# Seven quarter products in place of eight for a pointwise convolution inside a fused attention and cluster block

## The chip, the cores and the metric

One Trainium2 chip, one of its cores, float32 throughout. The metric is the device time of one execution in microseconds, and the times given are medians of repeated executions. The kernel is a two-layer network over four images of 256 channels and 64x64 pixels.

## The reference, cut to what matters

Layer 0 is self attention over the 4096 pixels of an image. Layer 1 is a cluster block followed by an MLP; the change touches only the end of layer 1:

```python
y = x + ls1 * cluster(group_norm(x), ...)
hdn = conv1x1(group_norm(y), mlp_w1, mlp_b1)          # 256 -> 1024
hdn = conv1x1(gelu(hdn), mlp_w2, mlp_b2)              # 1024 -> 256
y = y + ls2 * hdn
z = relu(batch_norm(y * dw_w, dw_g, dw_b, dw_m, dw_v))
z = relu(batch_norm(conv1x1(z, pw_w), pw_g, pw_b, pw_m, pw_v))   # 256 -> 256: the pointwise convolution
```

A `conv1x1` is a matrix product of a weight matrix with the pixels: here 256x256 by 256x4096 for an image.

## The kernel before

**Tiling.** An image's 4096 pixels go in eight blocks of 512 (`nb`), its channels in two halves of 128 partitions (`KC`). The third image leaves its last block over; it is worked off in the last image's cluster stage (`late_block`). TensorE is fed a stationary 128x128 weight tile and a moving tile of 256 or 512 columns, and each float32 product appears in the profile as two MATMUL rows.

**The order.** The whole body is under a manual schedule: each engine runs its instructions strictly in the order in which the program emits them, and waits on other engines by semaphore. The MLP of an image is the double loop at the end of `mlp`: for each block `nb`, for `j` in 0 to 3, `first(nb, j)` makes a quarter of the hidden layer and the second layer of the previous `j` is woven into it. The second layer is a Python generator, `second_by_seven`; `first` pulls products out of it at four points, `mo(0)` to `mo(3)`, and the tuple `slots` says how many at each. After a step without attention scores, `slots` is (0, 2, 2, 3); after one with, (3, 1, 2, 1).

**Strassen-like quarters.** Both MLP layers are already done with seven quarter products in place of eight: the weights and the 512-column operand are each cut in four (256 columns at a time), sums of the quarters are made, and seven products suffice. In `first`, `norm` makes the scaled input (VectorE, L1168) and four sums of its quarters (L1184 to L1187; on GpSimd, except for block 0). Three pairs of PSUM banks, `p`, `q` and `r`, take 2, 3 and 2 products. They come from a pool of two such pairs (`ps_s`), so a pair must have been read out before the next but one group can write. VectorE adds the products (`plus`, L1290), ScalarE copies one (L1307) and applies gelu (L1287).

**The second layer, product by product** (L1247). Call the hidden quarters of step `j` h1 to h4. Product 1 is w3 by h4, 2 is a12 by h3, 3 is a11 by h1; then GpSimd has rewritten the quarters, and 4 is w7 by h4, 5 is s1 by h2, 6 is s2 by h1, 7 is a22 by h3. GpSimd's four rewrites are h4 = h2 + h4 (L1252) and h2 = h2 − h1 (L1253), emitted after product 1, and h1 = h1 − h4 (L1256) and h3 = h1 + h3 (L1257), emitted after product 3. With (0, 2, 2, 3) products 1 and 2 come at `mo(1)`, 3 and 4 at `mo(2)`, 5 to 7 at `mo(3)`.

**The pointwise convolution.** `finish(nb)` adds the second layer's result to y, and two relus on ScalarE (L1336, emitted at the next block's `j` = 1) write the convolution's input over the block's own sums, `pairs[nb][:, 1]`. `last(nb)` (L1194) then runs at `j` = 2 of the next block: four 512-column products (L1206), two into each of two banks of one `ps_s` pair, two relus on ScalarE (L1215) and two output transfers on SyncE's queue (L1218). In an image's last block the previous block's convolution is called in the middle of `first` and uses two other banks; the last block's own convolution comes after the loop.

**What stands beside.** The sums for the next block, `norm(nb + 1)`, are scaled at `j` = 1; their GpSimd part is kept in `behind` and emitted inside the second layer of `j` = 1, after product 3's rewrites. Scores of the next image's attention are put in at `j` = 3 of each block (`score`; not in the last image, which has no next), and their running maxima run on VectorE as 128x512 maxima of two SBUF tiles (L372), called by `rest()` after `first` for `j` other than 1 and before it for `j` = 3.

Of the kernel before, what the change touches and what calls it, by code (L numbers as in the profile page):

```python
# [8 lines left out]
F32 = mybir.dt.float32  # L9
# [36 lines left out]
def attention_then_cluster_block(  # L46
# [977 lines left out]
    def late_block(b, y, gab):  # L1024
# [44 lines left out]
        def second(j, c):  # L1069
            if j == 0:  # L1070
                held["a", c] = ps_m.tile([P, NB], F32, tag="m", name=f"mol_{b}_{c}")
            nc.tensor.matmul(
                held["a", c],
                own_w["w2"][:, j, c * P : (c + 1) * P],
                hidden(j),
                start=(j == 0),
                stop=(j == HID // P - 1),
            )
            if j == HID // P - 1:
                t = work.tile([P, NB], F32, tag=f"w{c}", bufs=1, name=f"tl_{b}_{c}")  # L1080
                nc.scalar.activation(t, held["a", c], AF.Identity, scale=par("ls2", c))
                nc.gpsimd.tensor_tensor(held["y"][:, 0, c], held["y"][:, 0, c], t, ALU.add)
                nc.scalar.activation(
                    held["x"][:, 1, c],
                    held["y"][:, 0, c],
                    AF.Relu,
                    scale=dw_d[:, c : c + 1],
                    bias=dw_e[:, c : c + 1],
                )

        def last(c, k):
            if k == 0:
                held["p"] = ps_m.tile([P, NB], F32, tag="m", name=f"pwl_{b}_{c}")
            x = held["x"]
            nc.tensor.matmul(
                held["p"],
                wpw_s[:, k, c * P : (c + 1) * P],
                x[:, 1, k],
                start=(k == 0),
                stop=(k == KC - 1),  # L1100
            )
# [35 lines left out]
    def mlp(b, ys, stats2, fill, nxt, blocks, turned):  # L1137
# [15 lines left out]
        w3_s = swap.tile([P, h_n, P], F32, tag="mix", name=f"w2_3_{b}")  # L1153
# [8 lines left out]
        def norm(nb, eng):  # L1162


            pairs[nb] = pr = spool.tile([P, 2, KC, NB], F32, tag="s", name=f"xn2_{b}_{nb}")

            def scaled(k):
                nc.vector.tensor_scalar(  # L1168
                    pr[:, 0, k, :],
                    block(ys, k, nb),  # L1170
                    ga[:, k : k + 1],
                    gb[:, k : k + 1],
                    ALU.mult,
                    ALU.add,
                )


            e, f, g, h = quarters(pr[:, 0])
            t2, t4, t3, _ = quarters(pr[:, 1])
            scaled(0)  # L1180
            scaled(1)

            def factors():
                eng.tensor_tensor(f, f, e, ALU.subtract)  # L1184
                eng.tensor_tensor(t2, h, f, ALU.subtract)
                eng.tensor_tensor(t3, e, t2, ALU.subtract)
                eng.tensor_tensor(t4, t2, g, ALU.subtract)  # L1187

            return factors

        def quarters(t):
            return t[:, 0, :HB], t[:, 0, HB:], t[:, 1, :HB], t[:, 1, HB:]

        def last(nb, beside=False):  # L1194
            zs = pairs.pop(nb)

            if beside:
                ps = [
                    ps_m.tile([P, NB], F32, tag="m", name=f"pw{c}_{b}_{nb}") for c in range(KC)
                ]  # L1200
            else:
                two = ps_s.tile([P, 2, NB], F32, tag="s", name=f"pw_{b}_{nb}")
                ps = [two[:, c, :] for c in range(KC)]
            for c in range(KC):
                for k in range(KC):
                    nc.tensor.matmul(  # L1206
                        ps[c],
                        wpw_s[:, k, c * P : (c + 1) * P],
                        zs[:, 1, k, :],
                        start=(k == 0),  # L1210
                        stop=(k == KC - 1),
                    )
            for c in range(KC):
                o_s = zs[:, 0, c, :]
                nc.scalar.activation(  # L1215
                    o_s, ps[c], AF.Relu, scale=pw_s[:, c : c + 1], bias=pw_e[:, c : c + 1]
                )
                nc.sync.dma_start(out=ob[:, c, nb * NB : (nb + 1) * NB], in_=o_s)  # L1218

        norm(0, nc.vector)()  # L1220
        if nxt:
            nxt.q_block(0, nc.sync)

# [12 lines left out]
                    stop=(j == h_n - 1 and i != c),  # L1236
                )

        def second_by_seven(nb, acc, hs, j):


            h1, h2, h3, h4 = quarters(hs)
# [3 lines left out]
            def q(bank, half, a, t, start=False, stop=False):  # L1246
                return nc.tensor.matmul(  # L1247
                    bank[:, half * HB : (half + 1) * HB], a[:, j], t, start=start, stop=stop
                )

            yield q(x, 1, w3_s, h4, one)
            nc.gpsimd.tensor_tensor(h4, h2, h4, ALU.add)  # L1252
            nc.gpsimd.tensor_tensor(h2, h2, h1, ALU.subtract)  # L1253
            yield q(x, 0, a12_s, h3, stop=end)
            yield q(y, 0, a11_s, h1, one, end)
            nc.gpsimd.tensor_tensor(h1, h1, h4, ALU.subtract)  # L1256
            nc.gpsimd.tensor_tensor(h3, h1, h3, ALU.add)  # L1257
# [15 lines left out]
        def first(nb, j, todo, slots, meanwhile=lambda: None):  # L1273


            e, f, g, h = quarters(pairs[nb][:, 0])
            t2, t4, t3, _ = quarters(pairs[nb][:, 1])
            hs = work.tile([P, 2, NB], F32, tag=("t", "acc")[j % 2], bufs=1, name=f"hs_{b}_{nb}_{j}")
            h1, h2, h3, h4 = quarters(hs)
            act = AF.Gelu_apprx_tanh  # L1280
            lo, hi = pvc("b1", P, j), pvc("b1", P, j + 4)

            def banks(n):
                return ps_s.tile([P, 2, NB], F32, tag="s", name=f"h{n}_{b}_{nb}_{j}")

            def gelu(dst, src, bias):
                nc.scalar.activation(dst, src, act, bias=bias)  # L1287

            def plus(dst, ps, term):
                nc.vector.tensor_tensor(dst, ps, term, ALU.add)  # L1290
# [5 lines left out]
                    next(todo, None)  # L1296

            def product(out, w, x):
                nc.tensor.matmul(out, w[:, j * P : (j + 1) * P], x, start=True, stop=True)  # L1299


            mo(0)
            ps = banks("p")
            p, u = ps[:, 0, :HB], ps[:, 1, :HB]
            product(p, W_A, e)
            product(u, w_abcd, t2)
# [5 lines left out]
            product(q, W_CD, f)  # L1312
            product(u, w_bac, t3)
            product(v, w_bcd, h)
            plus(h3, u, h2)
            plus(h4, q, h3)
            gelu(h4, h4, hi)
            plus(h2, q, h2)
            plus(h2, v, h2)
            gelu(h2, h2, lo)  # L1320
            mo(2)
            meanwhile()
            ps = banks("r")
            p, u = ps[:, 0, :HB], ps[:, 1, :HB]
            product(p, W_B, g)
            product(u, W_D, t4)
            plus(h1, p, h1)
            gelu(h1, h1, lo)
            plus(h3, u, h3)
            gelu(h3, h3, hi)  # L1330
            mo(3)
            return hs

        def finish(nb, acc):
            def relu(c):
# [38 lines left out]

        hooks, drips, behind, maxima = [], [], [], []

        def hook():
            while hooks:  # L1380
# [4 lines left out]
                maxima.pop(0)()  # L1385

        acc, todo, slots = None, iter(()), (0,) * 4

        at = {(u, 3): u for u in range(7)} | {(7, 2): 7}
        if blocks < NBLK:  # L1390
# [2 lines left out]
        for nb in range(blocks):  # L1393
            end = nb == blocks - 1
            for j in range(4):
                if j == 3:
                    rest()
                pw = (lambda: last(nb - 1, True)) if end and j == 2 else lambda: None
                hs = first(nb, j, todo, slots, pw)
                if j != 1:  # L1400
                    rest()
# [166 lines left out]
```

## Time and profile before

| What | Value |
|---|---|
| Median of three executions | 3380.36 us (3377.95 to 3381.68) |
| The profiled execution, its own time | 3380.63 us |
| Span of its instructions | 3378.8 us |
| Granted TensorE clock, mean | 0.997 |
| TensorE busy | 3320.6 us |
| VectorE, ScalarE, GpSimd busy | 2151.6, 1659.6, 1833.4 us |
| DMA, mean over the span | 21 GB/s |
| Pointwise convolution L1206, MATMUL rows in all | 248 |
| One MLP block in the steady stretch (693.38 to 722.79) | 29.41 us, TensorE busy 29.27 |

The span is what the trace shows from the first to the last instruction; the execution's own time has 1.8 us more around it. Times inside the trace are microseconds from the span's start. MATMUL rows overlap, so the time of a product is read from the distance between starts, not from a row's length. Idle time of an engine other than TensorE costs nothing unless TensorE comes to wait for it. A trace can lack a few matmul records.

### The profile page before, as it was taken

What the parts mean: (1) busy time and instruction counts of PE and PEld (TensorE: products, weight loads), DVE (VectorE), ACT (ScalarE), POOL (GpSimd) and SP (SyncE); (2) the same over time, 40 slices, a digit from 0 to 9 for tenths busy, and PEclk for the clock granted to TensorE, in tenths of its full rate; (3) what the DMA queues carried; (4) which work ended last, traced back from release to release, by engine and by line L of the source; (5) the groups of instructions that cost most, each with busy time, mean ns of one, the idle gap of its engine ahead of it and who ended that gap; (6) DMA issues with size and microseconds to landing.
All of it is one profiled execution on the core that took longest, in us unless ns stands there. A gap on an engine that the chain in (4) does not pass through costs nothing.

```text
span 3378.8 us, 34064 instructions
## 1 busy us (share of the span) xinstructions
PE 3320.6 (98%) x12184; PEld 1778.9 (53%) x12184; DVE 2151.6 (64%) x3381; ACT 1659.6 (49%) x2184; POOL 1833.4 (54%) x1255
## 2 busy tenths in 40 slices
PE   8999999999999999999999999999999999999999
PEld 4434445777533344577744334467763344346786
DVE  4667664666666766466666676646656766765654
ACT  5545543444555554344455555434445555544444
POOL 2655666354365666545535566554534676573553
PEclk9999999999999999999999999999999999999999
DMA  2000002000000000100000000010000000010000
GB/s 71 13 13 11 15 7 86 4 13 19 26 13 13 13 13 22 71 4 19 19 22 13 10 13 13 22 70 4 19 26 13 13 13 13 10 39 1 13 19 26
DMA packets 43098, 70.95 MB, mean 21 GB/s; under 512 B 9680, under 2 KB 18480, under 8 KB 42928
## 3 DMA queue, kind: packets, MB, share of 16 engines
q1 hardware_dynamic: 38064, 61.94, 5.5%
q10 hardware_dynamic: 4608, 6.30, 0.8%
q8 instruction: 96, 1.57, 0.2%
q14 instruction: 74, 0.61, 0.1%
q0 software_dynamic: 256, 0.52, 0.1%
HBM read 43.46 MB, written 16.89 MB: 18 GB/s over the span
## 4 chain that ended last, share of the span: by engine, by line
PE 91%; DVE 7%; ACT 1%; issue 1%; DMA 0%; SPq 0%; ACTq 0%; DVEq 0%
PE av L473 53%; PE sc L359 8%; PE mo L1247 8%; PE hq L1299 4%; PE pw L1206 3%; PE hp L1299 3%; PE hr L1299 3%; PE vp L310 2%; PE fv L857 2%; DVE hs L1290 2%; PE mo L1231 1%; DVE x L1345 1%; DVE top L372 1%; PE op L978 1%; PE qp L329 0%
## 5 line engine op out<-in xcount | busy, mean ns | idle before, releaser
L473 PE MATMUL av<-s,v 128*128 128x512 f32 x4096 | 1819.2, 598 | 0.6 <-ACT s L463 0.6
L468 POOL TENSOR_TENSOR acc<-acc,s 128x1024 f32<-128x1024 f32 x448 | 1057.4, 2360 | 537.7 <-ACT s L463 518.9
L473 PEld LDWEIGHTS av<-s,v 128*128 128x128 f32 x4096 | 759.1, 190 | 1044.8 <-issue 1034.5
L463 ACT ACTIVATE s<-s 128x1024 f32<-128x1024 f32 x512 | 540.3, 1057 | 592.2 <-DVE s L460 549.5
L460 DVE TENSOR_TENSOR s<-s,mb 128x1024 f32<-128x1024 f32 x512 | 595.6, 1206 | 18.7 <-ACT mb L444 16.3
L381 DVE TENSOR_TENSOR top<-sc,top 128x1024 f32<-128x1024 f32 x196 | 239.4, 1222 | 374.6 <-PE sc L359 374.4
L1287 ACT ACTIVATE hs<-hs,pv_s 128x256 f32<-128x256 f32 x496 | 230.9, 503 | 350.3 <-DVE hs L1290 350.3
L1247 PE MATMUL mo<-hs,w 128*128 128x256 f32 x1512 | 385.9, 381 | 0.0
L377 ACT COPY s<-sc 128x1024 f32<-128x1024 f32 x224 | 224.9, 1004 | 225.7 <-PE sc L359 225.7
L1247 PEld LDWEIGHTS mo<-hs,w 128*128 128x128 f32 x1512 | 281.2, 190 | 59.0 <-issue 15.2
L359 PE MATMUL sc<-q,k 32*128 32x512 f32 x2048 | 294.7, 640 | 0.4 <-ACT s L382 0.4
L384 DVE TENSOR_TENSOR top<-sc,top 128x1024 f32<-128x1024 f32 x196 | 240.1, 1225 | 72.2 <-ACT s L377 59.5
L382 ACT COPY s<-sc 128x1024 f32<-128x1024 f32 x224 | 227.1, 1014 | 66.2 <-DVE top L379 36.2
L465 POOL TENSOR_TENSOR acc<-s 128x1024 f32<-128x1024 f32 x32 | 75.3, 2352 | 327.0 <-ACT s L463 327.0
L1252 POOL TENSOR_TENSOR hs<-hs 128x256 f32<-128x256 f32 x108 | 78.5, 727 | 305.7 <-PE mo L1247 201.5
L1290 DVE TENSOR_TENSOR hs<-hq,hs 128x256 f32<-128x256 f32 x496 | 198.6, 421 | 68.9 <-PE hq L1299 58.8
L1290 DVE TENSOR_TENSOR hs<-hp,hs 128x256 f32<-128x256 f32 x124 | 52.4, 423 | 267.4 <-ACT hs L1307 267.4
L359 PEld LDWEIGHTS sc<-q,k 32*128 32x128 f32 x2048 | 81.7, 182 | 182.5 <-issue 128.4
L1299 PE MATMUL hr<-xn,w 128*128 128x256 f32 x496 | 127.5, 379 | 0.3 <-DVE hs L1290 0.3
L310 PE MATMUL vp<-wv_s,x 128*128 128x256 f32 x512 | 123.4, 387 | 0.2 <-ACT v L318 0.2
L1206 PE MATMUL pw<-xn,wpw_s 128*128 128x512 f32 x248 | 112.1, 594 | 1.5 <-ACT xn L1336 1.5
L1256 POOL TENSOR_TENSOR hs<-hs 128x256 f32<-128x256 f32 x108 | 80.6, 746 | 57.6 <-PE mo L1247 55.7
(236 smaller groups left out, 3281.0 us busy)
## 6 DMA issues: line engine op xcount, KB each, us to landing
x<-in_x SPq DMA_DIRECT2D x32, 512.0 KB, 6.7
out<-xn SPq DMA_DIRECT2D x62, 256.0 KB, 2.1
w<-in_w SPq DMA_DIRECT2D x8, 1024.0 KB, 10.1
mr<-row_mx SPq DMA_DIRECT2D x28, 256.0 KB, 3.1
rden<-row_rd SPq DMA_DIRECT2D x28, 256.0 KB, 3.1
q<-q ACTq DMA_DIRECT2D x96, 64.0 KB, 2.0
mix<-in_wfv SPq DMA_DIRECT2D x8, 192.0 KB, 8.1
q<-q SPq DMA_DIRECT2D x24, 64.0 KB, 2.0
```

The source lines that it names most:

```text
L359: nc.tensor.matmul(halves[r // 2][:, r % 2, :], k_s[rows, g, :], q_s[rows, :], start=True, stop=True)
L381: nc.vector.tensor_tensor(top, halves[1], top, ALU.max)
L382: nc.scalar.copy(s[:, 2:4, :], halves[1])
L384: nc.vector.tensor_tensor(top, halves[0], top, ALU.max)
L460: nc.vector.tensor_tensor(sh, sh, mxs[nb].unsqueeze(1).to_broadcast([P, 2, NB]), ALU.subtract)
L463: nc.scalar.activation(sh, sh, AF.Exp)
L468: nc.gpsimd.tensor_tensor(acc, acc, s[:, 2 * h : 2 * h + 2], ALU.add)
L473: nc.tensor.matmul(av[c], own["v"][:, RG * g + quarter, c * P : (c + 1) * P], slots[u][:, quarter, :], start=(g == 0 and quarter == 0), st ...
L1247: return nc.tensor.matmul(bank[:, half * HB : (half + 1) * HB], a[:, j], t, start=start, stop=stop)
L1287: nc.scalar.activation(dst, src, act, bias=bias)
L1290: nc.vector.tensor_tensor(dst, ps, term, ALU.add)
L1299: nc.tensor.matmul(out, w[:, j * P : (j + 1) * P], x, start=True, stop=True)
```

## The change

The pointwise convolution of most blocks is turned to seven quarter products, in the form of `first`, whose inner part is taken out as a function `seven` and used by both. A new function `pointwise(nb)` calls it at the place of `last(nb - 1)`, `j` = 2 of blocks that are neither an image's first nor its last. The convolution's stored weights are changed in place at the start (two GpSimd operations), and three sums of them are made in each image's MLP, in the tile that holds w3.

The four sums of the convolution's operand (`factors`) are emitted on GpSimd inside the second layer of `j` = 1: the first ahead of product 1, the second ahead of product 3, the other two after product 3's rewrites. The next block's four sums, which stood there, move to the second layer of `j` = 2, after product 3's rewrites. `slots` is (3, 1, 2, 1) after the `j` = 2 of a block with a convolution.

An image's last two convolutions and the carried-over block stay at eight quarters (four 512-column products). Since the stored weights are changed, each of them gets one subtraction of the operand's halves: on GpSimd for the last but one and the carried-over block, on VectorE for the last.

```diff
+    pw_q = [wpw_s[:, k, h * P : (h + 1) * P] for k in range(KC) for h in range(2)]
+    nc.gpsimd.tensor_tensor(pw_q[1], pw_q[1], pw_q[3], ALU.add)
+    nc.gpsimd.tensor_scalar(pw_q[3], pw_q[3], -1.0, None, ALU.mult)
...
+                if c:
+                    x = held["x"]
+                    nc.gpsimd.tensor_tensor(held["y"][:, 1, 0], x[:, 1, 0], x[:, 1, 1], ALU.subtract)
...
-        def last(nb, beside=False):
+        def last(nb, beside, eng):
+
             zs = pairs.pop(nb)
+            eng.tensor_tensor(zs[:, 0, 1], zs[:, 1, 0], zs[:, 1, 1], ALU.subtract)
...
-                        wpw_s[:, k, c * P : (c + 1) * P],
-                        zs[:, 1, k, :],
+                        pw_q[2 * k + c],
+                        zs[:, 0, 1] if k and c else zs[:, 1, k],
...
+        def factors(eng, src, dst):
+
+
+            e, f, g, h = quarters(src)
+            t2, t4, t3, _ = quarters(dst)
+            yield eng.tensor_tensor(f, f, e, ALU.subtract)
+            yield eng.tensor_tensor(t2, h, f, ALU.subtract)
+            yield eng.tensor_tensor(t3, e, t2, ALU.subtract)
+            yield eng.tensor_tensor(t4, t2, g, ALU.subtract)
...
+        nc.gpsimd.tensor_tensor(pw_abcd, pw_q[1], pw_q[0], ALU.subtract)
+        nc.gpsimd.tensor_tensor(pw_bac, pw_abcd, pw_q[3], ALU.add)
+        nc.gpsimd.tensor_tensor(pw_bcd, pw_q[2], pw_abcd, ALU.subtract)
...
-        def second_by_seven(nb, acc, hs, j):
+        def second_by_seven(nb, acc, hs, j, own, ahead):
...
+            if j == 1:
+                next(own, None)
             yield q(x, 1, w3_s, h4, one)
             nc.gpsimd.tensor_tensor(h4, h2, h4, ALU.add)
             nc.gpsimd.tensor_tensor(h2, h2, h1, ALU.subtract)
             yield q(x, 0, a12_s, h3, stop=end)
+            if j == 1:
+                next(own, None)
             yield q(y, 0, a11_s, h1, one, end)
             nc.gpsimd.tensor_tensor(h1, h1, h4, ALU.subtract)
             nc.gpsimd.tensor_tensor(h3, h1, h3, ALU.add)
             if end:
                 early(nb, acc)
-            if behind:
-                behind.pop()()
+            if j == 1:
+                for _ in own:
+                    pass
+            if j == 2:
+                for _ in ahead:
+                    pass
             yield q(z, 0, w7_s, h4, one)
...
+        def pointwise(nb):
+            zs = pairs.pop(nb)
+
+            outs, spent = quarters(zs[:, 1]), quarters(zs[:, 0])
+            dst = outs[0], spent[0], spent[2], outs[3]
+
+            def done(i, src):
+                c = i // 2
+                rectified(c, outs[i], src)
+
+                if i % 2 == 0:
+                    leave(nb, c, zs[:, 1, c])
+
+            ws = (pw_q[0], pw_abcd, pw_q[1], pw_bac, pw_bcd, pw_q[2], pw_q[3])
+            seven(f"{nb}_pw", ws, zs[:, 1], zs[:, 0], dst, done, iter(()), (0,) * 4)
...
-                    if nb + 1 < blocks:
-                        behind.append(norm(nb + 1, nc.gpsimd))
+                    if not end:
+                        ahead = norm(nb + 1, nc.gpsimd)
+                        if nb:
+                            own = factors(nc.gpsimd, pairs[nb - 1][:, 1], pairs[nb - 1][:, 0])
+                        else:
+                            own = iter(())
                 elif j == 2 and nb and not end:
-                    last(nb - 1)
+                    pointwise(nb - 1)
...
-                    todo = second_by_seven(nb, acc, hs, j)
-                    slots = (3, 1, 2, 1) if scored else (0, 2, 2, 3)
+                    todo = second_by_seven(nb, acc, hs, j, own, ahead)
+                    slots = (3, 1, 2, 1) if scored or j == 2 and nb else (0, 2, 2, 3)
...
-        last(blocks - 1)
+        last(blocks - 1, False, nc.vector)
```

`seven` is the old inner part of `first` with the weights, the operand, the sums and the destinations as arguments: group `p` (2 products), a ScalarE copy and one VectorE addition; group `q` (3 products), four VectorE additions and two activations; group `r` (2 products), two VectorE additions and two activations. For the convolution the activation is the relu with its scale and bias, and nothing of the second layer is woven in.

More of the change, by code (lines that the diff above doesn't have):

```diff
@@ L1096, in last @@
                 held["p"],
-                wpw_s[:, k, c * P : (c + 1) * P],
-                x[:, 1, k],
+                pw_q[2 * k + c],
+                held["y"][:, 1, 0] if k and c else x[:, 1, k],
                 start=(k == 0),
@@ L1152, in mlp @@
         nc.gpsimd.tensor_tensor(w_bcd, W_B, w_abcd, ALU.subtract)
-        w3_s = swap.tile([P, h_n, P], F32, tag="mix", name=f"w2_3_{b}")
+        few = swap.tile([P, h_n + 3, P], F32, tag="mix", name=f"w2_3_{b}")
+        w3_s, (pw_bcd, pw_bac, pw_abcd) = few[:, :h_n], (few[:, h_n + i] for i in range(3))
         nc.gpsimd.tensor_tensor(w3_s, s2_s, a12_s, ALU.add)
@@ L1175, in scaled @@
                 )
-            e, f, g, h = quarters(pr[:, 0])
-            t2, t4, t3, _ = quarters(pr[:, 1])
             scaled(0)
             scaled(1)
[L1183 to L1189, printed above, removed]
+            return factors(eng, pr[:, 0], pr[:, 1])
         def quarters(t):
             return t[:, 0, :HB], t[:, 0, HB:], t[:, 1, :HB], t[:, 1, HB:]
-        def last(nb, beside=False):
+        def last(nb, beside, eng):
             zs = pairs.pop(nb)
+            eng.tensor_tensor(zs[:, 0, 1], zs[:, 1, 0], zs[:, 1, 1], ALU.subtract)
             if beside:
@@ L1207, in last @@
                         ps[c],
-                        wpw_s[:, k, c * P : (c + 1) * P],
-                        zs[:, 1, k, :],
+                        pw_q[2 * k + c],
+                        zs[:, 0, 1] if k and c else zs[:, 1, k],
                         start=(k == 0),
@@ L1213, in last, with rectified, leave @@
             for c in range(KC):
[L1214 to L1220, printed above, removed]
+                rectified(c, zs[:, 0, c], ps[c])
+                leave(nb, c, zs[:, 0, c])
+        def rectified(c, o_s, src):
+            nc.scalar.activation(
+                o_s, src, AF.Relu, scale=pw_s[:, c : c + 1], bias=pw_e[:, c : c + 1]
+            )
+        def leave(nb, c, o_s):
+            nc.sync.dma_start(out=ob[:, c, nb * NB : (nb + 1) * NB], in_=o_s)
+        def factors(eng, src, dst):
[5 more added lines that the diff above has]
+            yield eng.tensor_tensor(t4, t2, g, ALU.subtract)
+        for _ in norm(0, nc.vector):
+            pass
+        nc.gpsimd.tensor_tensor(pw_abcd, pw_q[1], pw_q[0], ALU.subtract)
+        nc.gpsimd.tensor_tensor(pw_bac, pw_abcd, pw_q[3], ALU.add)
+        nc.gpsimd.tensor_tensor(pw_bcd, pw_q[2], pw_abcd, ALU.subtract)
         if nxt:
@@ L1259, in second_by_seven @@
                 early(nb, acc)
-            if behind:
-                behind.pop()()
+            if j == 1:
[3 more added lines that the diff above has]
+                for _ in ahead:
+                    pass
             yield q(z, 0, w7_s, h4, one)
@@ L1273, in first, with gelu, seven, banks @@
         def first(nb, j, todo, slots, meanwhile=lambda: None):
-            e, f, g, h = quarters(pairs[nb][:, 0])
-            t2, t4, t3, _ = quarters(pairs[nb][:, 1])
             hs = work.tile([P, 2, NB], F32, tag=("t", "acc")[j % 2], bufs=1, name=f"hs_{b}_{nb}_{j}")
[L1279 to L1287, printed above, removed]
+            def gelu(i, src):
+                nc.scalar.activation(
+                    src, src, AF.Gelu_apprx_tanh, bias=pvc("b1", P, j + 4 * (i > 1))
+                )
+            ws = [
+                w[:, j * P : (j + 1) * P] for w in (W_A, w_abcd, W_CD, w_bac, w_bcd, W_B, W_D)
+            ]
+            seven(f"{nb}_{j}", ws, pairs[nb][:, 0], pairs[nb][:, 1], quarters(hs), gelu, todo, slots, meanwhile)
+            return hs
+        def pointwise(nb):
[9 more added lines that the diff above has]
+            seven(f"{nb}_pw", ws, zs[:, 1], zs[:, 0], dst, done, iter(()), (0,) * 4)
+        def seven(n, ws, src, sums, dst, act, todo, slots, meanwhile=lambda: None):
+            e, f, g, h = quarters(src)
+            t2, t4, t3, _ = quarters(sums)
+            h1, h2, h3, h4 = dst
+            w_p, w_u, w_q, w_u3, w_v, w_p2, w_u4 = ws
+            def banks(i):
+                return ps_s.tile([P, 2, NB], F32, tag="s", name=f"h{i}_{b}_{n}")
             def plus(dst, ps, term):
@@ L1298, in product @@
             def product(out, w, x):
-                nc.tensor.matmul(out, w[:, j * P : (j + 1) * P], x, start=True, stop=True)
+                nc.tensor.matmul(out, w, x, start=True, stop=True)
             mo(0)
@@ L1304, in first @@
             p, u = ps[:, 0, :HB], ps[:, 1, :HB]
-            product(p, W_A, e)
-            product(u, w_abcd, t2)
+            product(p, w_p, e)
+            product(u, w_u, t2)
             nc.scalar.copy(h1, p)
@@ L1311, in first @@
             q, u, v = ps[:, 0, :HB], ps[:, 1, :HB], ps[:, 0, HB:]
-            product(q, W_CD, f)
-            product(u, w_bac, t3)
-            product(v, w_bcd, h)
+            product(q, w_q, f)
+            product(u, w_u3, t3)
+            product(v, w_v, h)
             plus(h3, u, h2)
             plus(h4, q, h3)
-            gelu(h4, h4, hi)
+            act(3, h4)
             plus(h2, q, h2)
             plus(h2, v, h2)
-            gelu(h2, h2, lo)
+            act(1, h2)
             mo(2)
@@ L1324, in first @@
             p, u = ps[:, 0, :HB], ps[:, 1, :HB]
-            product(p, W_B, g)
-            product(u, W_D, t4)
+            product(p, w_p2, g)
+            product(u, w_u4, t4)
             plus(h1, p, h1)
-            gelu(h1, h1, lo)
+            act(0, h1)
             plus(h3, u, h3)
-            gelu(h3, h3, hi)
+            act(2, h3)
             mo(3)
-            return hs
         def finish(nb, acc):
@@ L1373, in finish @@
                 hooks.append(lambda c=c: relu(c))
-        hooks, drips, behind, maxima = [], [], [], []
+        hooks, drips, maxima = [], [], []
         def hook():
@@ L1387, in mlp @@
         acc, todo, slots = None, iter(()), (0,) * 4
+        own = ahead = iter(())
         at = {(u, 3): u for u in range(7)} | {(7, 2): 7}
@@ L1397, in mlp @@
                     rest()
-                pw = (lambda: last(nb - 1, True)) if end and j == 2 else lambda: None
+                pw = (lambda: last(nb - 1, True, nc.gpsimd)) if end and j == 2 else lambda: None
                 hs = first(nb, j, todo, slots, pw)
```

## The prediction

> **What bounds the kernel now.** I read the page first: how busy each engine is, and the chain of waits that ended last.
>
> ```profile
> PE 3320.6 (98%) x12184; PEld 1778.9 (53%) x12184; DVE 2151.6 (64%) x3381; ACT 1659.6 (49%) x2184; POOL 1833.4 (54%) x1255
> ...
> PE 91%; DVE 7%; ACT 1%; issue 1%; DMA 0%; SPq 0%; ACTq 0%; DVEq 0%
> PE av L473 53%; PE sc L359 8%; PE mo L1247 8%; PE hq L1299 4%; PE pw L1206 3%; PE hp L1299 3%; PE hr L1299 3%; PE vp L310 2%; PE fv L857 2%; DVE hs L1290 2%; PE mo L1231 1%; DVE x L1345 1%; DVE top L372 1%; PE op L978 1%; PE qp L329 0%
> ...
> L1206 PE MATMUL pw<-xn,wpw_s 128*128 128x512 f32 x248 | 112.1, 594 | 1.5 <-ACT xn L1336 1.5
> ```
>
> TensorE is busy 98% of the span and 91% of the chain. So a product taken away is worth its whole time, and a wait put ahead of TensorE costs its whole time. The convolution itself is 3% of the chain. The other engines are half idle on average, which says nothing of one stage. Hence the second view, the timeline of one image's third block (nb=2), around the place where the change lands:
>
> ```profile
> 722.79 1.07 PE L1247 MATMUL mo<-hs,w 128*128 128x256 f32 x4
> 723.02 1.50 ACT L1336 ACTIVATE xn<-x,dw_e,dw_d 128x512 f32<-128x512 f32 x2
> ...
> 723.53 0.73 POOL L1252 TENSOR_TENSOR hs<-hs 128x256 f32<-128x256 f32 x1 [2.65 <-PE mo L1247]
> ...
> 724.34 0.72 POOL L1253 TENSOR_TENSOR hs<-hs 128x256 f32<-128x256 f32 x1
> ...
> 725.74 0.73 POOL L1256 TENSOR_TENSOR hs<-hs 128x256 f32<-128x256 f32 x1 [0.68 <-PE mo L1247]
> ...
> 726.54 0.73 POOL L1257 TENSOR_TENSOR hs<-hs 128x256 f32<-128x256 f32 x1
> 726.72 1.46 PE L1247 MATMUL mo<-hs,w 128*128 128x256 f32 x6
> ...
> 727.23 0.73 POOL L1184 TENSOR_TENSOR xn<-xn 128x256 f32<-128x256 f32 x1
> 727.60 2.04 DVE L372 TENSOR_TENSOR top<-top,s 128x512 f32<-128x512 f32 x2
> ...
> 728.02 3.60 PE L1206 MATMUL pw<-xn,wpw_s 128*128 128x512 f32 x8
> 728.04 1.05 POOL L1185 TENSOR_TENSOR xn<-xn 128x256 f32<-128x256 f32 x1
> ...
> 731.45 0.59 PE L1299 MATMUL hp<-xn,w 128*128 128x256 f32 x2
> ```
>
> Columns: start, duration, engine, line, operation. A product is two MATMUL rows. I call the start of the first line S (722.79). TensorE runs products 1 and 2 of the second layer at S and S+0.43, 3 and 4 at S+2.21 and S+2.64, 5 to 7 at S+3.93, S+4.36 and S+4.80 (the x6 line, 0.43 apart). GpSimd makes what they read: h4 (L1252) for product 4, h2 (L1253) for 5, h1 (L1256) for 6, h3 (L1257) for 7. h1 ends at 726.47, S+3.68, so product 6 has 0.68 us in hand; h3 ends at 727.27, S+4.48, so product 7 has 0.32. That 0.32 us is what the change spends. The separate starts show the same pattern, within 0.02 us, for nb=1 to 5 of every image; at nb=6 of the first two images products 5 to 7 are 0.43 later.
>
> [...] so I take spacings. L1252 to L1253, where the second waits for the first, is 0.80; L1257 to L1184, which does not, is 0.69. [...] beside L372 the GpSimd L1185 takes 1.05, where most of its kind take 0.73.
>
> **The change part by part.**
>
> *Removed from TensorE.* Four 512-column products take 731.45 − 728.02 = 3.43 us. Seven 256-column ones at 0.432 (the spacing of L1247 and L1299) take 3.03. Gain 0.40 us. The next hq product waits for the old 128x512 relus (23 waits on L1215, 0.08 us of TensorE each, as 733.18 to 733.69 instead of 0.43); that goes, since the new evictions are shorter and earlier. Gain 0.48 in all. It happens at nb=1 to 6 of three images and nb=1 to 5 of the third: 23 places, 11.0 us. An image's last two convolutions stay at eight quarters.
>
> *Added on GpSimd, and moved.* The four sums for the next block (L1184 to L1187) move from this stage to the next one; the pointwise operand's four take their place, but two of them are set ahead of the second layer's own. The new order in j=1's second layer is: own f, h4, h2, own t2, h1, h3, own t3, own t4. Own f reads the first relu (L1336). The two relus take 0.75 each, and the first one's record ends at 723.82, S+1.03. GpSimd follows ACT by about 0.08 (L1082 starts at 3135.93 after ACT's 3135.16+0.69). So f starts at S+1.11; h4 0.69 later, S+1.80; h2 at S+2.60 (0.80); t2 at S+3.28 (the second relu is done by S+1.73); h1 at S+3.97; h3 at S+4.77. With 0.73 each and 0.08 to reach TensorE: product 4 can start at S+2.61 (due 2.64, just in time), 5 is free, 6 at S+4.78 (due 4.36), 7 at S+5.58 (due 4.80). Everything behind product 7 in TensorE's queue slips by 0.78 us. Net for a place: 0.78 − 0.48 = +0.30.
>
> *The tie at S+4.8.* In three images VectorE starts its L372 at S+4.81, 0.04 us after h3's start by my sum. Where GpSimd starts 0.11 ahead (L1253 at 3317.57 against L1345 at 3317.68) it keeps its 0.73 and VectorE is stretched to 1.16. If VectorE is first instead, h3 waits for nearly all of one two-input read, some 0.6 (L1185 comes 0.44 after L372 and still loses 0.32). Then the slip is about 1.4, at 17 of the 23 places; the last image has no L372. I take GpSimd first; both ends go into the range.
>
> *The seven products after that.* Bank pairs: the third group needs the first one's pair, free after a ScalarE copy and a VectorE addition, 0.35 + 0.42 after the u product, and the second group's 1.30 us of products covers that. The copy overwrites e, so it waits for own t3, S+5.46 to about 6.8[...]; the first group ends at S+6.87, so nothing. VectorE gets seven additions of 0.42, 2.9 us, into an idle stretch of 4.89 (with one row less of L372, at 703.98). ScalarE gets a 0.35 copy and four 0.5 relus for two of 0.75. After them three second-layer products come first, 1.30 us, and cover the last additions. The next block's moved sums end about 4 us later than j=2's h3, still ahead of their use where a score stands between. Nothing here.
>
> *Small ones.* Last image, nb=0: no score stands between, and t2 is late. h1 stays at 3172.73, h3 3173.54, f 3174.23, t2 3175.03 to 3175.76, reaching TensorE at 3175.84; its product is due at 3175.44: +0.4 us. An image's last convolution gets a VectorE subtraction (a two-input 128x512 L372 takes 0.68 alone) behind two 1.15 us subtractions of L460: 895.17+2.3+0.68 = 898.15, and its product is due near 898.2: nothing, at worst 0.7 for each of three images. The one before gets a GpSimd subtraction of 1.27 (as L485) while GpSimd is idle and 3.5 us of products run. At the start, the weights' two GpSimd operations stand behind the q transfers at 17.35 to 21.48, wait for a transfer that lands at 24.8, and GpSimd is next needed after the first exponentials, past 45. Three 128x128 sums go where GpSimd idles 7.80 us. The block carried over to the last image gets a GpSimd subtraction after its second relu, 3140.79, ahead of the weight sums L1150 to L1154, which then end 2.2 later, at 3147.2; the first that TensorE reads is due at 3146.95 and made by 3143.4, the last at 3151.66. Two output transfers per place stay on SP's queue, with the same bytes. All nothing.
>
> **Sum.** 23 × 0.30 = 6.9, plus 0.4: 7.3 us on the profiled execution's own 3380.63 (span 3378.8), which is 0.3 above the median 3380.36. Rounded up by a microsecond for the nb=6 places[...]: about 3389.
>
> **The rivals.**
> 1. *VectorE wins the tie* (chance 0.32): 17 × 0.6 = 10.2 more, about 3399. For: my order rests on 0.04 us. Against: GpSimd is ahead by the sum.
> 2. *GpSimd's chain is hidden* (0.14): this ends on the other side. The whole gain of 11.0 stands and the time is about 3370. The mechanism is own f starting before the first relu bound or h1 starting by about S+3.5; it decides from a chain 0.8 us shorter than my sum. Against: L1336's end and the in-order queue leave no room for that.
> 3. *Half hidden* (0.12): the slip is about 0.4, near the gain; 3380 to 3383. It would need shorter spacings than 0.69 and 0.80, which appear nowhere.
> 4. *The change isn't seven quarters at all:* the program order shows seven products; no chance given.
>
> **Numbers.** Forecast as summed 0.42. Within 0.2% (6.8 us) is what a measurement of this kernel can't tell from no change; the forecast's edge lies close to it, so about 0.07 of its 0.42 falls inside. Slower 0.35 + 0.32 = 0.67, same 0.07 + 0.12 = 0.19, faster 0.14. The range goes from 3381 to 3401: from half hidden to the tie lost with the small costs in full.
>
> **What would show it.** Right: L1247's products 6 and 7 of j=1 waiting on GpSimd, 23 times, 0.8 us of gap together; the convolution's products at 0.432 each; block period 29.41 (the repeat of S, 752.21 − 722.79) grown to about 29.7, or 30.3 if VectorE wins. Wrong: a block period of 28.9 and no TensorE wait on GpSimd; or waits of TensorE on VectorE in the seven products, which I priced at nothing.

## The result and the profile after

| What | Before | After |
|---|---|---|
| Median (six executions each) | 3381.02 us (3377.95 to 3385.21) | 3409.27 us (3405.58 to 3410.22) |
| The profiled execution, its own time | 3380.63 us | 3409.36 us |
| Span | 3378.8 us | 3407.6 us |
| Granted TensorE clock, mean | 0.997 | 0.995 |
| One MLP block, images 0 to 2 / last image | 29.41 / 28.03 us | 30.29 / 28.44 us |

The changed kernel is slower: ratio 1.0081, 95% interval 1.0068 to 1.0094. Between the two profiled executions lie 28.7 us, where the forecast had 8.4. The page of the changed kernel, its busy times and its chain of waits:

```profile
PE 3337.4 (98%) x12322; PEld 1807.4 (53%) x12322; DVE 2220.3 (65%) x3546; ACT 1684.4 (49%) x2253; POOL 1919.1 (56%) x1366
...
PE 85%; DVE 8%; POOL 3%; ACT 2%; issue 1%; DMA 0%; SPq 0%; ACTq 0%; DVEq 0%; POOLq 0%
```

TensorE is still busy 98% of the time, with less to multiply. The chain says more: TensorE's share of it fell from 91% to 85%, and GpSimd, which was not in it, holds 3%. So new waits stand in TensorE's path. The view of waits names them (engine, line, what is waited for, then total us, number, longest):

```profile
PEld mo L1266 <- POOL hs L1279: 12.3, 21, 0.6
PEld mo L1266 <- POOL hs L1280: 10.6, 21, 0.5
PEld sc L363 <- DVE hs L1342: 10.2, 36, 0.8
```

The first two are the second layer's products 6 and 7, waiting for GpSimd, as forecast. The third, scores waiting for VectorE's additions, is not in the forecast at all. (The kernel before has it twice, for 1.4 us.) The timeline of the third block shows the first two; PEld is TensorE's weight load:

```profile
726.28 1.07 PE L1266 MATMUL mo<-hs,w 128*128 128x256 f32 x4
...
727.38 0.73 POOL L1230 TENSOR_TENSOR xn<-xn 128x256 f32<-128x256 f32 x1 [3.01 <-ACT xn L1387]
...
728.07 0.73 POOL L1273 TENSOR_TENSOR hs<-hs 128x256 f32<-128x256 f32 x1
...
728.88 0.73 POOL L1274 TENSOR_TENSOR hs<-hs 128x256 f32<-128x256 f32 x1
...
729.57 0.73 POOL L1231 TENSOR_TENSOR xn<-xn 128x256 f32<-128x256 f32 x1
...
730.25 0.73 POOL L1279 TENSOR_TENSOR hs<-hs 128x256 f32<-128x256 f32 x1
730.25 0.59 PE L1266 MATMUL mo<-hs,w 128*128 128x256 f32 x2
...
731.03 1.50 PE L1266 MATMUL mo<-hs,w 128*128 128x256 f32 x4 [0.19 <-POOL hs L1279]
731.06 0.72 POOL L1280 TENSOR_TENSOR hs<-hs 128x256 f32<-128x256 f32 x1
731.13 1.21 DVE L376 TENSOR_TENSOR top<-top,s 128x512 f32<-128x512 f32 x1
...
731.84 0.30 PEld L1266 LDWEIGHTS mo<-hs,w 128*128 128x128 f32 x2 [0.51 <-POOL hs L1280]
...
732.37 0.59 PE L1351 MATMUL hp_pw<-xn,wpw_s 128*128 128x256 f32 x2
```

S is 726.28 here. GpSimd's own f stands at S+1.10, h4 at 1.79, h2 at 2.60, own t2 at 3.29, h1 at 3.97, h3 at 4.78: the sum in the prediction, within 0.02 us. Product 6 starts at S+4.75 and product 7 (weights loaded at 731.84) at S+5.56; the convolution starts at S+6.09, where it started at S+5.23 before. So the slip is 0.86 us, here and at 20 more of the 23 places. At nb=6 of the first two images, where product 5 is the one that comes late (S+5.01 instead of S+4.36), it is 0.66. GpSimd was 0.07 ahead of VectorE's L376, kept its 0.72, and VectorE was stretched (1.21 instead of 0.68).

Two more places hold the rest. The scores of that block, in TensorE's timeline, first after and then before:

```profile
740.53 1.03 PE L1351 MATMUL hr<-xn,w 128*128 128x256 f32 x4
741.40 0.59 PE L1266 MATMUL mo<-hs,w 128*128 128x256 f32 x2
741.92 1.61 PE L363 MATMUL sc<-q,k 32*128 32x512 f32 x8
743.47 1.56 PE L1266 MATMUL mo<-hs,w 128*128 128x256 f32 x6
```

```profile
706.00 1.03 PE L1299 MATMUL hr<-xn,w 128*128 128x256 f32 x4
706.87 1.46 PE L1247 MATMUL mo<-hs,w 128*128 128x256 f32 x6
708.25 1.14 PE L359 MATMUL sc<-q,k 32*128 32x512 f32 x8
709.33 1.56 PE L1247 MATMUL mo<-hs,w 128*128 128x256 f32 x6
```

A score's rows took 1.08 us before (708.25 to 709.33) and take 1.55 now. One second-layer product stands between group r (hr) and the score; before it was three (the x6 line). And the start of an image's MLP, after and then before, all engines:

```profile
654.91 0.54 DVE L263 TENSOR_SCALAR ga_gn<-pc_s,rstd_gn 128x2 f32<-128x2 f32 x1
654.96 0.46 POOL L1237 TENSOR_TENSOR w<-wpw_s 128x128 f32<-128x128 f32 x1
...
655.49 0.49 DVE L264 SCALAR_TENSOR_TENSOR gb_gn<-ga_gn,dv_gn,pc_s 128x2 f32<-128x2 f32 x1
655.50 0.45 POOL L1238 TENSOR_TENSOR w<-w,wpw_s 128x128 f32<-128x128 f32 x1
...
656.71 0.70 PE L1351 MATMUL hp<-xn,w 128*128 128x256 f32 x2 [1.49 <-DVE xn L1176]
...
658.55 1.05 PE L1351 MATMUL hq<-xn,w 128*128 128x256 f32 x2
```

```profile
654.27 0.23 DVE L259 TENSOR_SCALAR ga_gn<-pc_s,rstd_gn 128x2 f32<-128x2 f32 x1
654.54 0.22 DVE L260 SCALAR_TENSOR_TENSOR gb_gn<-ga_gn,dv_gn,pc_s 128x2 f32<-128x2 f32 x1
...
655.39 0.70 PE L1299 MATMUL hp<-xn,w 128*128 128x256 f32 x2 [0.81 <-DVE xn L1168]
...
657.24 0.59 PE L1299 MATMUL hq<-xn,w 128*128 128x256 f32 x2
```

VectorE operations on two elements a partition take 0.54 and 0.49 beside GpSimd's weight sums (L1237 to L1239), where they took 0.23 and 0.22 without them. TensorE waits 1.49 instead of 0.81 for its first product. And then the products themselves run at half speed (hq 1.05 instead of 0.59; granted clock 0.50 from 658.55 to 661.96, 1.00 there before). The kernel before already shows such a stretch in the same place: its L246, a VectorE operation on one element a partition, took 1.09 us in the first image and ended 0.02 after GpSimd's L1152, a sum of 1.26.

Where the 28.7 us lie, from the difference of starts of the same TensorE instruction in both traces. (From here on, "the statistics" means the start of VectorE's BATCH_NORM_AGGREGATE in an image's normalization, L239 before and L243 after.)

| Stretch | us |
|---|---|
| MLP blocks, images 0 to 2 (17 places with a convolution) | 16.2 |
| MLP blocks, last image (6 places, 0.4 for its block 0) | 2.9 |
| MLP starts, from the statistics to the first second-layer product, four images | 2.0 + 0.7 + 2.1 + 2.7 |
| Elsewhere: a half-speed stretch in image 2's cluster stage (6.83 us from 2314.02, 3.41 before), the first transfers | 2.0 |

A block period grew by 0.88 us in images 0 to 2 and by 0.41 in the last image, which has no scores. The difference, 0.47, is the score rows' 1.55 − 1.08.

### The profile page after: what moved, and what is told of

It reads as the page before. It is cut to its first block, busy times and chain, and to the rows that moved or that the text cites. A ratio compares the mean times of both kernels' runs of the same rounds, so it can differ in the third digit from the quotient of the medians.

```text
span 3407.6 us, 34726 instructions
## 1 busy us (share of the span) xinstructions
PE 3337.4 (98%) x12322; PEld 1807.4 (53%) x12322; DVE 2220.3 (65%) x3546; ACT 1684.4 (49%) x2253; POOL 1919.1 (56%) x1366
## 4 chain that ended last, share of the span: by engine, by line
PE 85%; DVE 8%; POOL 3%; ACT 2%; issue 1%; DMA 0%; SPq 0%; ACTq 0%; DVEq 0%; POOLq 0%
PE av L477 53%; PE sc L363 8%; PE mo L1266 6%; PE hq L1351 3%; PE vp L314 2%; PE hp L1351 2%; PE fv L861 2%; PE hr L1351 2%; DVE hs L1342 2%; PE mo L1250 1%; DVE x L1396 1%; ACT hs L1306 1%; PE hq_pw L1351 1%; PE pw L1206 1%; DVE top L376 1%
## 5 line engine op out<-in xcount | busy, mean ns | idle before, releaser
L1266 PE MATMUL mo<-hs,w 128*128 128x256 f32 x1512 | 401.7, 385 | 6.1 <-POOL hs L1279 3.9
L363 PE MATMUL sc<-q,k 32*128 32x512 f32 x2048 | 302.5, 640 | 0.5 <-ACT s L386 0.5
L1273 POOL TENSOR_TENSOR hs<-hs 128x256 f32<-128x256 f32 x108 | 78.5, 727 | 209.3 <-PE mo L1266 101.0
L314 PEld LDWEIGHTS vp<-wv_s,x 128*128 128x128 f32 x512 | 93.5, 190 | 26.2 <-issue 11.2
L1351 PEld LDWEIGHTS hr<-xn,w 128*128 128x128 f32 x496 | 94.9, 192 | 20.7 <-issue 4.8
```

Of the source, the lines that this page charges most:

```text
L314: nc.tensor.matmul(vps[0][:, i % 2, :], xs[i * P // XT][:, k, o : o + P], wv_s[:, k, :], start=(k == 0), stop=(k == KC - 1),)
L363: nc.tensor.matmul(halves[r // 2][:, r % 2, :], k_s[rows, g, :], q_s[rows, :], start=True, stop=True)
L1266: return nc.tensor.matmul(bank[:, half * HB : (half + 1) * HB], a[:, j], t, start=start, stop=stop)
L1351: nc.tensor.matmul(out, w, x, start=True, stop=True)
```

## The experiments

The kernel before was measured again beside each set of runs: 3385.20 us beside the first four, 3383.74 beside the others. Ratios are to that; where I compare with the changed kernel's 3409.27, which was measured beside 3381.02, a few us are uncertain, and the block periods and distances of the traces, which repeat to 0.02 us, carry the verdict.

**The weight sums,** moved into block 0, where no small VectorE operation that TensorE waits for stands beside them:

```diff
-        nc.gpsimd.tensor_tensor(pw_abcd, pw_q[1], pw_q[0], ALU.subtract)
...
+            if nb == 0 and j == 0:
+                nc.gpsimd.tensor_tensor(pw_abcd, pw_q[1], pw_q[0], ALU.subtract)
...
```

> The changed kernel, with the three weight sums (L1237 to L1239) moved from the start of the MLP into block 0's first step, behind h3's rewrite on GpSimd. If they hold VectorE's normalization at the MLP's start (from the normalization's statistics to the first hidden product 5.65 us after the change, 4.97 before), this stretch is 4.97 again in the first three images and the TensorE clock dips behind it go: 4 to 8 us less than the changed kernel, about 3403. If the late start and the dips have another cause: no change, within 2 us of 3409. The block period stays 30.29 by both.

Measured 3403.94 us (ratio to before 1.0062, 1.0047 to 1.0077), 5.3 less than the changed kernel, inside what was expected. From the statistics to the first product: 4.97 us in the first three images, as before the change, where the changed kernel has 5.63 to 5.65; blocks 30.30 and 28.45, unchanged.

**The slots.** The three second-layer products put back between group r and the score:

```diff
-                    slots = (3, 1, 2, 1) if scored or j == 2 and nb else (0, 2, 2, 3)
+                    slots = (3, 1, 2, 1) if scored else (3, 0, 1, 3) if j == 2 and nb else (0, 2, 2, 3)
```

> The changed kernel, with slots (3, 0, 1, 3) in place of (3, 1, 2, 1) after j = 2, so that three second-layer products stand between hr's products and the scores as before the change. If the scores wait for hr's banks to be read out, the eight score rows take 1.08 us again in place of 1.55, the block period of the first three images falls from 30.29 to 29.8, the last image's stays 28.44, and the time falls by 17 x 0.48 = 8 us to about 3401. If the slower scores have another cause, 3409 stays.

Measured 3397.55 us (1.0043, 1.0026 to 1.006). That is 11.7 less than the changed kernel where 8 were expected, but the four executions spread from 3392.32 to 3402.91, so the verdict rests on the period: 29.83 in images 0 to 2, and 28.45 in the last, unchanged. TensorE's timeline of this kernel at the place shown above:

```profile
739.48 1.03 PE L1351 MATMUL hr<-xn,w 128*128 128x256 f32 x4
740.34 1.46 PE L1266 MATMUL mo<-hs,w 128*128 128x256 f32 x6
741.73 1.14 PE L363 MATMUL sc<-q,k 32*128 32x512 f32 x8
742.80 1.56 PE L1266 MATMUL mo<-hs,w 128*128 128x256 f32 x6
```

With three products behind hr the rows take 1.07 again, with the seven products still there. So it is the distance between hr and the score, not the seven products, that made scores slow.

**The operand's first two sums on VectorE.** Own f and t2 go from GpSimd's queue to VectorE's, behind the normalization of the next block:

```diff
-            yield eng.tensor_tensor(f, f, e, ALU.subtract)
-            yield eng.tensor_tensor(t2, h, f, ALU.subtract)
+            yield lead.tensor_tensor(f, f, e, ALU.subtract)
+            yield lead.tensor_tensor(t2, h, f, ALU.subtract)
...
-            if j == 1:
-                next(own, None)
...
+                            next(own)
+                            next(own)
```

> The changed kernel, with the operand's first two sums (f, t2) on VectorE, right after the next block's normalization, and only t3 and t4 on GpSimd, behind h3. If GpSimd's longer queue is what holds products 6 and 7, they are back at 0.43 and 0.87 after product 5, and each of the 23 places gains 0.75 to 0.86: block period 29.45 and 27.6 (last image), time 17 to 20 us less, about 3391. If the hidden bound is VectorE, the period stays or grows, since VectorE gets two operations more.

Measured 3394.04 us (1.0038, 1.0026 to 1.0051). Products 5 to 7 start at S+3.98, 4.41 and 4.84; the block period is 29.45 and 27.60, 0.84 less than the changed kernel's in both. The convolution starts at S+5.27 instead of 6.09, so all but 0.04 of the slip is gone, and with the score repaired too a period of 29.41 − 0.43 is left: the change's own gain. In all it is 15.2 us less than the changed kernel, short of the 17 to 20 expected: at nb=6 of the first two images the convolution came later than in the changed kernel (S+7.68 and 6.86 instead of 6.32).

**All three together.** Block 0, which has no convolution of its own, also gets its sums for the next block back in the second layer of `j` = 1.

> All three edits together, and the next block's sums of block 0 back at j = 1. If the three causes are separate, the gains add: 30 to 36 us less than the changed kernel, 3373 to 3379, below the kernel before; block period 28.95. If one only uncovers another, the gain is well short of the sum, and the time stays above 3381.

Measured 3380.15 us (0.9987, 0.9979 to 0.9996). The block periods are 28.98 and 27.60, each 0.43 less than before the change, which over 23 places would be 10 us. The medians show five, and the result lies above the 3373 to 3379 that were expected. The same comparison of starts showed where the others went: the place at nb=6 lost 0.74 us against before in the second image instead of gaining 0.43, and 3.25 in the first, where a half-speed stretch follows it; and the last image's first product with w_abcd came 10.17 us after the statistics, where it had been 8.84. The first is the repair's own doing: at nb=6 the next block's normalization waits for the relus, and the two sums moved to VectorE stood behind it and ahead of the addition that frees group p's banks. In the second image:

```profile
1683.09 1.13 PE L1349 MATMUL hr<-xn,w 128*128 128x256 f32 x4 [1.37 <-DVE hs L1340]
```

The second is the carried-over block's subtraction, and belongs to the change.

**The carried-over block without its subtraction.** Its second output half takes three products with the original weight quarter in place of two with a difference:

```diff
+    pw_d = const.tile([P, P], F32, name="pw_d")
+    nc.gpsimd.tensor_copy(pw_d, pw_q[3])
...
-                if c:
-                    x = held["x"]
-                    nc.gpsimd.tensor_tensor(held["y"][:, 1, 0], x[:, 1, 0], x[:, 1, 1], ALU.subtract)
...
+            if k and c:
+                nc.tensor.matmul(held["p"], pw_q[3], x[:, 1, 0], start=False, stop=False)
...
-                held["y"][:, 1, 0] if k and c else x[:, 1, k],
+                x[:, 1, k],
```

> The changed kernel, with the carried-over block's pointwise convolution put back without a subtraction on GpSimd: a copy of the weight quarter w11 is kept, and its second output half takes three products (q1 by x0, -w11 by x0, w11 by x1) in place of two with a difference; nothing of the computation is left out. My theory after the result: the 1.27 us GpSimd subtraction pushed the last image's four weight sums beside VectorE's normalization[...], so that the first product that needs w_abcd and t2 comes 10.15 us after the statistics' aggregate, where it came 8.84 before. Then here that distance is 8.8 to 8.9, the GpSimd sums start right after L1086, and the time is 1.3 us less than the changed kernel's 3409.3 (and up to 3 less if the half-clock stretch of 3.4 us behind that wait goes too). Rival, as my prediction had it: the subtraction costs nothing there, the distance stays near 10 and the time stays at 3409. The blocks' period stays 30.3 and 28.4 for both.

Measured 3405.88 us (1.0065, 1.005 to 1.008), 3.4 less than the changed kernel; its four executions spread over 8.7 us, so here too the distances decide. The changed kernel's timeline at the last image's MLP start, all engines:

```profile
3163.71 1.27 POOL L1096 TENSOR_TENSOR yl<-xl 128x512 f32<-128x512 f32 x1 [0.92 <-ACT xl L1087]
...
3166.25 2.98 DVE L1176 TENSOR_SCALAR xn<-x,ga_gn,gb_gn 128x512 f32<-128x512 f32 x2
3166.28 1.26 POOL L1158 TENSOR_TENSOR w_bac<-w_abcd,w 128x512 f32<-128x512 f32 x1
...
3168.91 1.44 POOL L1162 TENSOR_TENSOR w<-w,w 128x512 f32<-128x512 f32 x1
3169.15 1.48 DVE L1230 TENSOR_TENSOR xn<-xn 128x256 f32<-128x256 f32 x1
...
3171.37 1.19 PE L1351 MATMUL hp<-xn,w_abcd 128*128 128x256 f32 x2 [2.71 <-DVE xn L1231]
```

The subtraction (L1096) delays the weight sums until they stand beside VectorE's normalization, which takes 2.98 us for two instead of 1.0, and L1230 1.48 instead of 0.42. TensorE waits 2.71. Without the subtraction the weight sums start 1.52 us after the statistics instead of 3.71 (1.79 before), and the product with w_abcd comes after 9.08 instead of 10.14. That is 0.2 more than I expected: TensorE itself is late there and VectorE no longer, since the carried-over block has one product more, which takes 0.86 us (3163.61 to 3164.47), behind four rows that took 3.22 us (from 3160.39) where eight take 3.43 at full speed.

**The two mis-priced parts put into the kernel before.** First the three weight sums alone, which nothing reads (the cut lines make room for them in the tile of w3):

```diff
...
         norm(0, nc.vector)()
+        nc.gpsimd.tensor_tensor(pw_abcd, pw_q[1], pw_q[0], ALU.subtract)
+        nc.gpsimd.tensor_tensor(pw_bac, pw_abcd, pw_q[3], ALU.add)
+        nc.gpsimd.tensor_tensor(pw_bcd, pw_q[2], pw_abcd, ALU.subtract)
```

> The kernel before, with only the three 128x128 weight sums added on GpSimd at the place where the change puts them (the MLP's start, behind the first block's own sums on VectorE); nothing reads them. Theory: beside VectorE's small normalization steps they cost 0.67 us in each of the first three images (aggregate to first product 5.64 instead of 4.97) and up to 0.7 in the last, so 2.0 to 2.7 us in all, ratio 1.0006 to 1.0008; a half-clock stretch behind the wait would add up to 1.7 per image. Rival (the prediction's own price): they lie in GpSimd's idle time and cost nothing, 4.97 stays. The blocks' period stays 29.41 and 28.03 for both.

Measured 3388.95 us against 3383.74 (1.0014, 1.0007 to 1.0021): 5.2 us, about twice what I had expected without the clock. From the statistics to the first product it is 5.63 or 5.64 in the three images. From that product to the second layer's first it is 7.21, 7.32 and 7.73 us, where it is 6.04 before. The window of 5 us behind the wait, in this kernel (third number from the right: granted clock):

```profile
655.00:660.00 5.00, 4.18 (x12) 3.00 (x13) 2.84 (x8) 1.43 (x3) 0.10 (x1) 0.66 0.00 0
```

The kernel before has 1.00 there. So the sums cost 0.67 us an image by the stretched operations, and 1.2 to 1.7 more by the clock.

Then the slots alone, with the eight-quarter convolution:

```diff
-                    slots = (3, 1, 2, 1) if scored else (0, 2, 2, 3)
+                    slots = (3, 1, 2, 1) if scored or j == 2 and nb else (0, 2, 2, 3)
```

> The kernel before, eight quarter convolution kept, with only the slots (3, 1, 2, 1) also after a block's second step, as the change has them; same arithmetic. Theory: the scores then stand one second-layer product behind group r, so their second half's banks wait for the two VectorE additions of r: a score's eight rows take 1.55 us instead of 1.08, the period of a block in the first three images goes from 29.41 to 29.88, the last image (no scores) stays 28.03, and the time grows by 17 x 0.47 = 8 us, ratio 1.0024. Rival (prediction: nothing there): rows 1.08, period 29.41, ratio 1.000.

Measured 3390.09 us (1.002, 1.0013 to 1.0027); period 29.81 in images 0 to 2, 27.95 in the last. The score in TensorE's timeline of this kernel:

```profile
706.39 1.03 PE L1299 MATMUL hr<-xn,w 128*128 128x256 f32 x4
707.26 0.59 PE L1247 MATMUL mo<-hs,w 128*128 128x256 f32 x2
707.78 1.61 PE L359 MATMUL sc<-q,k 32*128 32x512 f32 x8
709.33 1.56 PE L1247 MATMUL mo<-hs,w 128*128 128x256 f32 x6
```

1.55 us again, without any seven-product convolution, and 6.4 us in all. I expected a period of 29.88; it is 0.08 less because three products now stand between the convolution and the next hq, whose wait for the old relus (0.08) goes, in the last image too.

**A version that keeps the gain.** All three repairs, the carried-over block as above, and at an image's last place the normalization moved to the second step, ahead of the convolution, and the running maxima behind it:

```diff
-                        ahead = norm(nb + 1, nc.gpsimd)
+                        if nb != blocks - 2:
+                            ahead = norm(nb + 1, nc.gpsimd)
...
+                    if nb == blocks - 2:
+                        ahead = norm(nb + 1, nc.gpsimd)
                     pointwise(nb - 1)
+                    if nb == blocks - 2:
+                        rest()
```

> All three repairs of the run with everything together, and two more: the carried-over block without its subtraction (as in w5_late), and in the last place of an image (the block before its last) the next block's normalization on VectorE moved from the first step, where it waits for the relus and stands with the two moved sums ahead of the additions, to the second step ahead of the convolution. Theory: that place loses 0.74 us against before in the run with everything together and should gain 0.43 as the other places do, so 1.2 less per image; with 1.3 less at the last image's start the time falls from 3380.2 to about 3374, and to 3371 if two half-clock stretches go; ratio to before 0.996 to 0.998. Block periods stay 28.98 and 27.60. Rival: these places are not what keeps the gain away; then 3380 stays, and TensorE's clock is the cause.

Measured 3374.97 us against 3383.74 (0.9972, 0.9962 to 0.9983). As expected, about 3374. The last place of the second image gained 0.97 us of the 1.2, since a wait of 0.30 for a VectorE addition remains in its next step. This is the one version that beats the kernel before by more than 0.2%.

## Why the prediction was right and where it was wrong

- *Added on GpSimd, and moved; the tie.* Right. The chain's starts hold to 0.02 us, and GpSimd was ahead, by 0.06 to 0.08 us, at all 15 places where there was a tie (at nb=6 of the first two images L376 came 1.3 later). One term was mis-sized: the slip is 0.86, not 0.78. Products 6 and 7 came at S+4.75 and 5.56, as summed, but the convolution starts 0.53 behind product 7 and not 0.43: as I read it, where the weight load itself waits (731.84 above), it is no longer hidden behind the product ahead of it. Over 21 places 1.7 us.
- *Removed from TensorE.* Right. The convolution takes 3.06 us from its first product to the next second-layer product, where 3.03 was forecast; the net of slip and gain is 0.41 a place (last image's period), where 0.30 was.
- *The seven products after that.* "After them three second-layer products come first, 1.30 us, and cover the last additions ... Nothing here" is the step that failed. It is true of the convolution's own additions at 20 of 23 places; at three, its last group waited 0.28 to 0.37 us for VectorE, 1.0 together. But the new slots take those three products from the end of the step, where they stood between group r and the score. I followed what the three products cover at their new place and not what they had covered at the old one. The two runs that set the slots alone show it, by a period of 0.46 less and 0.40 more (0.47, less the wait of 0.08 that goes too): 17 places, 0.47 us each, 8.0 us.
- *Small ones.* "Three 128x128 sums go where GpSimd idles 7.80 us ... All nothing" is the second failed step. GpSimd's idleness was real and beside the point: VectorE, on TensorE's path just then, paid. The sums cost 5 us (both runs), 2.0 of it by the stretched operations and the rest by half-speed stretches. The carried-over subtraction, priced from when TensorE reads the weight sums, cost 2.7 at the last image's start in the same way, 1.3 by the stretched operations and 1.4 by a half-speed stretch: the sums were in time, but VectorE's normalization took 2.98 us beside them instead of 1.00. Of the 20.3 us between forecast and measurement the scores and the MLP starts make 15.5. The 0.4 at the last image's block 0 was there (24.47 to 24.94).
- *Operations side by side.* The prediction had both sides from the trace: GpSimd's L1185 took 1.05 us beside L372 instead of 0.73, and VectorE's L1345 took 1.16 beside L1253, which kept its 0.73. Into the sums it went for GpSimd alone. What cost time was VectorE's side: beside GpSimd's sums its operations took 0.54 us for 0.23, 2.98 for 1.00 (L1176) and 1.48 for 0.42 (L1230).
- *The rivals.* VectorE did not win the tie; GpSimd's chain was not hidden. The block period of 30.3 that was named as VectorE's sign did come (30.29), but by chance: it is 29.41 + 0.41 + 0.47, from other terms. None of the rivals held the two causes that made the difference, 8 us at the scores and 7.5 at the MLP starts.

It remains to say when a half-speed stretch comes. After MLP starts with a distance of 4.97 us it came in none of 15 cases (five traces), and after 5.24 to 5.65 us in 11 of 15 (five other traces; in the changed kernel at 658.55 and 2348.15). In each of the ten traces all changes of the granted clock lie on a grid of 3.413 us, to within 0.005 us, and the grid falls differently on the program in each. No window ahead of these 11 was idle: TensorE multiplied in a part of each. Two windows of that grid with the one behind each, at the MLP starts of the changed kernel's first and second image (first number behind the comma: TensorE busy; third from the right: granted clock):

```profile
655.14:658.55 3.41, 1.28 (x5) 0.78 (x5) 3.27 (x8) 2.07 (x3) 1.15 (x3) 1.00 0.00 0
658.55:661.96 3.41, 3.41 (x10) 2.69 (x9) 1.15 (x4) 0.37 (x1) 0.00 (x0) 0.50 0.00 0
1498.23:1501.64 3.41, 1.92 (x8) 1.15 (x8) 2.67 (x7) 2.26 (x4) 2.38 (x4) 1.00 0.00 0
1501.64:1505.05 3.41, 2.77 (x13) 2.20 (x12) 2.38 (x7) 0.39 (x2) 0.00 (x0) 1.00 0.00 0
```

The same waits were cut by the grid in two ways: in the first image most of them fell into one window, in the second they were shared between two. A row's busy time is modelled, so as an estimate I charged each MATMUL row its spacing at full clock instead, 0.216 us for 256 columns. Of some 9,770 full-speed windows in the ten traces (their first part, 15 us before the change and 17 after, has no record of the clock), 62 were followed by half speed. In all 62 TensorE multiplied for at most 0.38 of the window, and in none of those that were followed by full speed for less than 0.37; between the two both came. At the 30 MLP starts the emptiest window has 0.23 to 0.32 in ten of the 11 that fell (0.38 in the other), and 0.37 to 0.43 in the 19 that did not. In the first image of the changed kernel the emptiest window went from 0.38 before the change to 0.25 with the sums' longer wait, and the clock fell; in the second, where the grid shared the wait between two windows, it stayed at 0.38, and the clock held. Why the clock falls is not shown; this is read from the ten traces, and no run moved the grid.

## What to carry to other kernels

When products are moved to cover something, ask also what they covered where they stood. And when work is put on an idle engine, look at who runs beside it in those microseconds: here GpSimd operations in GpSimd's idle time stretched VectorE's on the critical path (0.54 us for 0.23, 2.98 for 1.00). A gain of 0.4 us a place was real; where the sums, the three products and the subtraction were placed decided its sign, not the seven products themselves.

## What the hardware showed that I had not expected

- VectorE operations on two elements a partition took 0.54 and 0.49 us beside 128x128 GpSimd sums of 0.46 and 0.45, 0.23 and 0.22 without them, and one on a single element 1.09 beside a sum of 1.26. Each of the three ended 0.02 or 0.03 us after the GpSimd operation beside it.
- The granted TensorE clock was 0.50 in stretches mostly of 3.41 us or twice that; hq then took 1.05 us instead of 0.59. The kernel before has 24 us of it in the profiled execution, the changed one 34, the best one 26. A short added wait ahead of a busy stretch cost several times its length: in the kernel before with the sums, 0.67 us became 1.8 to 2.4 in an image. In the ten traces all 62 falls came behind a window of the 3.41 us grid in which TensorE multiplied for at most 0.38 of the time, by the estimate above.
- The eight rows of a score took 1.08 us when nothing held their banks, and 1.55 when their weight loads waited for the two additions of group r: the first half for one, the second half, 0.19 us, for the other. Their starts then lay within 1.03 us (741.92 to 742.95) instead of 0.56 (708.25 to 708.81).
